# Two ResNet-style blocks in fp32: loads at the start, scale rows, V tiles by column pairs, a positions buffer and the last output chunk

## The chip, the cores and the metric

The kernel runs on one core of one Trainium2 chip. The time is the device time of one execution in microseconds (us). TensorE (PE) does the matmuls, VectorE (DVE) and ScalarE (ACT) the elementwise work, GpSimd (POOL) and SyncE (SP) mostly issue DMAs. ACT can issue DMAs too: an issue stands in its own queue, in order with its other work, so an issue that waits holds up the instructions behind it.

## The reference, cut to what matters

x has 16 images of 1024 channels and 32x32 pixels, all in fp32. Two layers follow each other.

```python
# layer 0
h = relu(bn(conv1x1(x, w_conv1)))                    # 1024 -> 256
q, k, v = relu(bn(conv1x1(h, wq))), relu(bn(conv1x1(h, wk))), bn(conv1x1(h, wv))
# per pixel, heads of 8 channels, 3x3 neighbourhood:
attn = softmax(sum_d q * (unfold3x3(k) + pos))       # 9 logits
h = relu(bn(sum_9 unfold3x3(v) * attn))
x = relu(bn3(conv1x1(h, w_conv3)) + x)               # 256 -> 1024, residual
# layer 1
o = relu(bn(conv1x1(x, w1)))                         # 1024 -> 256
o = relu(bn(conv3x3(o, w2)))                         # 256 -> 256
x = relu(bn(conv1x1(o, w3)) + x)                     # 256 -> 1024, residual
```

pos is pos_h + pos_w, one number per channel and neighbour. Each bn of layer 1 is a scale gamma / sqrt(var + eps) and a shift.

## The kernel before, in words

**Stages.** A list of stages (L917) sets the order of TensorE. For image b: C is layer 0's first convolution, Q the products for k and q and the position terms, V those for v. F is "fused": layer 0's last convolution, its residual, and at once layer 1's first convolution. W is the 3x3 convolution for a group of four images in Winograd form (W0, W4, W8, W12). U is layer 1's last convolution with its residual. The list begins P0 P1 P2 P3 F0 (P stands for C, Q, V) and ends W12 U11 U12 U13 U14 U15. In a stage of 1x1 convolution one chunk is 128 channels of one image, 512 KB, and its matmuls take about 3.4 us.

**VectorE.** The attention of an image (`attend`), the Winograd input transform of an image (`transform`) and, at the start, the Winograd form of w2 (`winograd_weights`, L251) and the folding of bn3's and layer 1's scales into the weights w3 and u3 (`scale_weights`) are jobs. A planner (class Side, L820) puts their instructions between those of the stages, by clocks of its own. Within an engine the resulting order is fixed.

**Queues.** SyncE issues the weights (`more_weights`, six buffers, in a fixed order), the stores of Winograd weights, of transformed images ("v") and of attention results. GpSimd issues the loads of x, of stored residuals and of V tiles (`more_loads`, L305: one list in fixed order, eight buffers, next when one is free), the stores of results (L397), of q (L490) and of the positions (L484). The eight x chunks of image 0 are issued on ACT's queue (L322). Each DMA takes a semaphore in turn, one of eight for SyncE and ACT together and one of eight for GpSimd, and its issue waits until the DMA before it on that semaphore has landed.

**What the change touches.**
- The beginning. L89 loads the parameters (`par`). L150 to L160 compute layer 1's norms from them (one square root on ACT, nine small operations on VectorE), L181 to L194 a small table of positions. Then `at_first` issues the x chunks of image 0, the taps of w2 and the unscaled w3 and u3 (GpSimd), four pieces of weights (SyncE: both halves of w1, the first in two parts, then wqk and wv), registers the two first jobs, and calls `scale_rows`.
- `scale_rows` (L217) brings the 1024 scales of each layer, which lie in SBUF as 128 partitions by 8 columns, into one row of 1024 that is the same in every partition: a store to DRAM with a transpose (1024 pieces of 4 bytes), then a load that reads the row 128 times ("scales"). `scale_weights` multiplies (L231) and stores the result.
- `winograd_weights` works on ACT and VectorE by turns (L259 to L270) and stores each row of products as `uw`; the stage Q of image 0 runs beside it.
- Q (`project`, L422): k and q are normed by ACT (L444) and stored. `positions` (L465) multiplies q with the position table (L470), lets ACT copy the sums from PSUM (L479) into q's first half, `q[:, 0, :]`, and stores them (L484). That copy overwrites q, so it waits until q's own store (L490) has read it.
- `transform` (L649) makes the six column forms of an image in three pairs, (1,2), (3,4), (0,5), each form in a zpool buffer, and stores them (L690) in DRAM. After an image's last pair it counts the image (`forms`), and a V tile is loaded once all four images are counted. V tiles are named (i, part); part 0 holds columns 1 and 3, part 1 columns 2 and 4, part 2 columns 0 and 5.
- zpool has three buffers: the scales, the forms v, the trees of the softmax and the copies z of a Winograd stage (L746) share them.
- `Expand.result` (L388) adds shift and relu to a chunk by one ACT operation over its 1024 pixels (L396) and stores it on GpSimd's queue (L397). The last chunk of all is chunk 7 of image 15.

Of the kernel before, what the change touches and what calls it, by code (L numbers as in the profile page):

```python
# [10 lines left out]
ALU = mybir.AluOpType  # L11
# [60 lines left out]
def sa_bottleneck_kernel(ctx: ExitStack, tc: tile.TileContext, x, w1t, wqkvt, w3t, u1t, u2t, u3t, params, out):  # L72
# [74 lines left out]
    bn_a = const.tile([P, _NBN], F32, tag="bn_a", name="bn_a")  # L147
    bn_r = const.tile([P, _NBN], F32, tag="bn_r", name="bn_r")
    bn_t = const.tile([P, _NBN], F32, tag="bn_t", name="bn_t")
    nc.vector.tensor_scalar(bn_a, bn_block("L1_conv_v1"), EPS, None, ALU.add)  # L150
    nc.scalar.activation(bn_r, bn_a, AF.Sqrt)

    nc.vector.reciprocal(bn_t, bn_r)
    nc.vector.tensor_mul(bn_t, bn_t, bn_a)
    nc.vector.tensor_add(bn_t, bn_t, bn_r)
    nc.vector.tensor_scalar(bn_t, bn_t, 0.5, None, ALU.mult)
    nc.vector.reciprocal(bn_r, bn_t)
    nc.vector.tensor_mul(bn_inv, bn_r, bn_block("L1_conv_g1"))
    nc.vector.tensor_mul(bn_t, bn_inv, bn_block("L1_conv_m1"))
    nc.vector.tensor_sub(bn_sh, bn_block("L1_conv_b1"), bn_t)  # L160


    members = const.tile([P, G], F32, tag="members", name="members")
# [14 lines left out]

    offsets = const.tile([P, NW, NPOS], F32, tag="offsets", name="offsets")
    pos = const.tile([P, NW, G, NPOS], F32, tag="pos", name="pos")  # L180
    for n in range(NW):  # L181
        for half, name in enumerate(("L0_conv_pos_h", "L0_conv_pos_w")):
            nc.vector.tensor_tensor(
                offsets[:, n, 2 * half : 2 * half + 2],
                col(name, 3 * n, 2),
                col(name, 3 * n + 2).to_broadcast([P, 2]),
                ALU.subtract,
            )
        nc.vector.tensor_tensor(
            pos[:, n],  # L190
            members.unsqueeze(2).to_broadcast([P, G, NPOS]),
            offsets[:, n].unsqueeze(1).to_broadcast([P, G, NPOS]),
            ALU.mult,
        )  # L194

# [19 lines left out]
    def scale_rows():  # L217

        for which, scale in enumerate((col("L0_conv_bn3_s", 0, NC), bn_inv[:, 2 * NW : 2 * NW + NC])):
            row = dram.tile([NC, P], F32, tag=f"row{which}", name="row")  # L220
            nc.sync.dma_start(row.rearrange("o p -> p o"), scale)
            t = zpool.tile([P, HW], F32, tag="z", name="scales")
            nc.sync.dma_start(t, AP(row.tensor, row.offset, [[0, P], [1, C]]))
            scales.append(t)

    def scale_weights():

        for which in range(2):
            for half in range(2):
                t = scaled[which, half]  # L230
                nc.vector.tensor_tensor(  # L231
                    t, t, scales[which][:, halves(half)].unsqueeze(1).to_broadcast([P, NW, HALF]), ALU.mult
                )
                nc.sync.dma_start(ws[which, half], t)
                yield 1.3


# [67 lines left out]
    def more_loads():  # L305

        while credits[0] and loads:
            kind, b, c = loads[0]
            if kind == "V":
                if forms.get(b, 0) < NK:  # L310
                    return
                src = form_room(b)[c[0], c[1]].rearrange("p k j e -> p (k j e)")
            elif kind == "r":
                if (b, c) not in stored:
                    return
                src = stored[b, c]
            else:
                src = x[b, c * P : (c + 1) * P, :]
            t = xpool.tile([P, NK * 2 * PART], F32, tag="x", name=f"{kind}_{b}_{c}".translate(str.maketrans(" ,", "__", "()")))
            t = t if kind == "V" else t[:, :HW]  # L320

            (nc.scalar if kind == "x" and b == 0 else nc.gpsimd).dma_start(t, src)  # L322
            loaded[loads.pop(0)] = t
            credits[0] -= 1
# [34 lines left out]
    class Expand:  # L359
# [28 lines left out]
        def result(self, o, to):  # L388
            t = self.tiles.pop(o)
            ps, to_ = self.ahead.pop(o), t  # L390

            if self.kind == "s":
                ps, to_ = ps.rearrange("p (n j) -> p j n", j=4), t.rearrange("p (j n) -> p j n", j=4)
            else:
                ps, to_ = ps.rearrange("p (j n) -> p n j", j=4), t.rearrange("p (n j) -> p n j", j=4)
            nc.scalar.activation(to_, ps, RELU, bias=self.shift(o), scale=1.0)  # L396
            nc.gpsimd.dma_start(to, t)  # L397
            return t
# [23 lines left out]
    def project(b):  # L422

        h = hidden.pop(b)

        def conv(which, n):
            ps = psum.tile([P, HW], F32, tag="ps", name="ps")
            name, at = ("wqk", which * WID) if which < 2 else ("wv", 0)
            key, at = piece(name, 0), at + n * P
            for half in range(2):  # L430
                for m in range(NW):
                    nc.tensor.matmul(  # L432
                        ps[:, halves(half)],
                        pieces[key][:, m, at : at + P],
                        h[:, m, halves(half)],
                        start=(m == 0),
                        stop=(m == NW - 1),
                    )
            if n == NW - 1 and which:
                done_with(key)  # L440
            return ps

        def norm(dst, src, name, n, func):
            nc.scalar.activation(  # L444
                dst, src, func,
                bias=col(f"L0_conv_{name}_b", n), scale=col(f"L0_conv_{name}_s", n),
            )

        def halo(name, which, func):

            room, backs[name] = by_quarter(name, b, HALO, HEAD_DIM)
            for n in range(NW):
                norm(inside(kp, n), rows(conv(which, n)), name, n, func)

                block = kp[:, n]
                nc.sync.dma_start(
                    room[n], AP(block.tensor, block.offset, [block.ap[0], [JROWS * PW, NJ], [1, HALO]])
                )
                yield CHUNK

        backs = relaid[b] = {}
        q = hpool.tile([P, NW, HW], F32, tag="h", name=f"q_{b}")
        room, backs["q"] = by_quarter("q", b, JPIX, HEAD_DIM)

        def positions():  # L465

            ps = psum.tile([P, HW], F32, tag="ps", name="ps")
            for half in range(2):
                for n in range(NW):
                    nc.tensor.matmul(  # L470
                        ps[n * G * NPOS : (n + 1) * G * NPOS, halves(half)],
                        pos[:, n].rearrange("p g t -> p (g t)"),
                        q[:, n, halves(half)],
                        start=True,
                        stop=True,
                    )

            by_offset = q[:, 0, :]
            nc.scalar.activation(by_offset, ps, AF.Identity)  # L479

            room, backs["pos"] = by_quarter("pos", b, JPIX, NPOS)
            by_offset = by_offset.rearrange("p (j w) -> p j w", j=NJ)
            for n in range(NW):
                nc.gpsimd.dma_start(room[n], by_offset[n * G * NPOS : (n + 1) * G * NPOS])  # L484

        k = halo("bnk", 1, RELU)
        yield next(k)
        for n in range(NW):
            norm(q[:, n, :], conv(0, n), "bnq", n, RELU)
            nc.gpsimd.dma_start(room[n], q[:, n, :].rearrange("p (j w) -> p j w", j=NJ))  # L490
            yield CHUNK
        yield next(k)
        positions()
        side.add(b)
        written.add(("qk", b))
        relay("qk", b)
        yield 2.5
        for n, cost in enumerate(halo("bnv", 2, AF.Identity)):
            if n:
                written.add(("v", b))  # L500
                relay("v", b)
            yield cost
# [146 lines left out]
    def transform(b, src):  # L649
# [35 lines left out]
        for make, two in pairs:  # L685
            v = [zpool.tile([P, HW], F32, tag="z", name="v")[:, : NI * PART] for _ in two]
            make([u.rearrange("p (l c) -> p l c", c=TR) for u in v], [t[:, :, at : at + TR] for at in PLACES])
            for j, u in zip(two, v):
                at = COLUMNS.index(j)
                nc.sync.dma_start(  # L690
                    room[:, at // 2, :, b % NK, at % 2].rearrange("i p e -> p i e"),
                    u.rearrange("p (i e) -> p i e", i=NI),
                )

            yield 4.3, 0.0 if b % NK == NK - 1 else 3.0
        forms[b - b % NK] = forms.get(b - b % NK, 0) + 1
        more_loads()

    def winograd_conv(b):

# [412 lines left out]
    made = []  # L1113

    def at_first():
        more_loads()
        for m in range(NW):
            load_taps(m)
        load_scaled()
        for _ in range(4):  # L1120
            more_weights()
        side.first(winograd_weights(), 24.0, 0.0)
        side.first(scale_weights(), 24.0, 0.0)
        scale_rows()
        hooks["conv1", 2, 0] = clear_hidden

    at_first()
# [42 lines left out]
```

## Time and profile before

The median of three runs is 2446.26 us (2446.19 to 2449.38). The profiled run took 2443.2 us, its span is 2441.2 us.

| engine | busy us | share | instructions |
|---|---|---|---|
| TensorE | 2388.6 | 98% | 6144 |
| VectorE | 2076.8 | 85% | 1631 |
| ACT | 918.2 | 38% | 873 |
| GpSimd | 463.2 | 19% | 851 |

A busy share is an average over all stages; where TensorE waits, and for whom, is told by the view of waits and by the timeline. In a timeline the columns are start, length, engine, line and operation, "out<-in", shapes, count, and in brackets the idle time before with what ended it. "q" behind an engine's name is its queue of DMA issues. Lines of one kind that follow each other are put together: "x8" are eight of them, and the length then spans all of them.

### The profile page before, as it was taken

Reading aid. Unit: us, or ns where it says so; the run is one execution under the profiler, and the core shown is the slowest. Engines: PE = TensorE matmul, PEld = TensorE weight load, DVE = VectorE, ACT = ScalarE, POOL = GpSimd, SP = SyncE. Lnnn points to the kernel's source line nnn. Section 1 sums busy time; section 2 is a strip of 40 time slices with the busy share of each in tenths; the row PEclk is TensorE's granted clock in tenths of the full one; section 3 lists DMA queues with packets and bytes.
Section 4 is the critical chain, followed back from the end, with each engine's and each line's share of the span. In section 5 each row is a group of like instructions: output and inputs, shape, how many; then the busy total and the mean of one; then the engine's idle time right before and its main releaser. Section 6 shows DMA issues by size and latency. Waiting matters only on the chain.

```text
span 2441.2 us, 18393 instructions
## 1 busy us (share of the span) xinstructions
PE 2388.6 (98%) x6144; PEld 1152.5 (47%) x6144; DVE 2076.8 (85%) x1631; ACT 918.2 (38%) x873; POOL 463.2 (19%) x851
## 2 busy tenths in 40 slices
PE   7999999999999999999999999999999999998998
PEld 3444444444466444444466444444466444434843
DVE  3899998999989999998989999899989999964700
ACT  2323142333122564433122564334222553443265
POOL 2121111111121222111111222111121221112122
PEclk9999999999999999999999999999999999999999
DMA  9967787878697899797888899797798897799788
GB/s 316 381 232 267 287 257 246 266 274 268 251 345 256 310 324 355 260 316 266 254 310 284 287 319 354 239 316 280 250 348 283 285 339 264 275 306 322 280 263 270
DMA packets 307693, 708.37 MB, mean 290 GB/s; under 512 B 22544, under 2 KB 176144, under 8 KB 298896
## 3 DMA queue, kind: packets, MB, share of 16 engines
q0 software_dynamic: 118816, 470.86, 54.4%
q1 hardware_dynamic: 187488, 232.10, 29.3%
q10 hardware_dynamic: 1296, 4.24, 0.5%
q8 instruction: 49, 0.80, 0.1%
q14 instruction: 44, 0.36, 0.0%
HBM read 432.10 MB, written 275.03 MB: 290 GB/s over the span
## 4 chain that ended last, share of the span: by engine, by line
PE 64%; DVE 15%; DMA 13%; issue 5%; ACT 2%; POOL 1%; SPq 0%; ACTq 0%; POOLq 0%; DVEq 0%
PE ps L346 26%; PE ps L377 19%; PE ps L432 10%; DMA out_dram<-r 8%; PE ps L723 8%; DVE acc L590 3%; DVE acc L603 3%; DVE prod L539 2%; DVE v L654 1%; DVE form L654 1%; DMA row<-par 1%; PE ps L470 1%; DVE prod L544 1%; DMA bnk<-kp 1%; POOL r L322 1%
## 5 line engine op out<-in xcount | busy, mean ns | idle before, releaser
L377 PE MATMUL ps<-a,w 128*128 128x512 f32 x1024 | 461.3, 596 | 4.9 <-ACT a L629 4.6
L346 PE MATMUL ps<-s,u 128*128 128x512 f32 x1024 | 458.3, 593 | 2.7 <-ACT s L396 2.7
L346 PE MATMUL ps<-x,w 128*128 128x512 f32 x1024 | 444.5, 595 | 14.2 <-DMA x<-in_x_dram 14.2
L377 PE MATMUL ps<-y,u 128*128 128x512 f32 x1024 | 442.6, 593 | 6.2 <-ACT ps L370 6.2
L590 DVE TENSOR_TENSOR acc<-e,bnv 128x2048 f32<-128x2048 f32 x144 | 327.5, 2284 | 3.6
L539 DVE TENSOR_TENSOR prod<-qc,bnk 128x2048 f32<-128x2048 f32 x144 | 324.1, 2287 | 1.7
L396 ACT ACTIVATE s<-ps,par 128x1024 f32<-128x1024 f32 x128 | 142.5, 1113 | 471.4 <-PE ps L377 402.9
L346 PEld LDWEIGHTS ps<-x,w 128*128 128x128 f32 x1024 | 195.5, 191 | 260.0 <-issue 259.0
L377 PEld LDWEIGHTS ps<-a,w 128*128 128x128 f32 x1024 | 195.3, 191 | 252.8 <-issue 242.2
L377 PEld LDWEIGHTS ps<-y,u 128*128 128x128 f32 x1024 | 194.2, 190 | 252.7 <-issue 236.4
L346 PEld LDWEIGHTS ps<-s,u 128*128 128x128 f32 x1024 | 194.7, 190 | 248.0 <-issue 237.9
L603 DVE TENSOR_TENSOR acc<-acc 128x2048 f32<-128x2048 f32 x128 | 293.4, 2292 | 4.4
L432 PE MATMUL ps<-h,wqk 128*128 128x512 f32 x512 | 225.9, 595 | 5.4 <-ACT h L975 5.2
L397 POOL DMA_DIRECT2D r<-s x128 | 68.6, 536 | 630.5 <-ACT s L396 600.4
L396 ACT ACTIVATE r<-ps,bn_sh 128x1024 f32<-128x1024 f32 x128 | 141.8, 1108 | 106.5 <-PE ps L377 106.1
L544 DVE TENSOR_TENSOR prod<-prod 128x2048 f32<-128x2048 f32 (+1 forms) x80 | 166.2, 2077 | 2.4
L432 PEld LDWEIGHTS ps<-h,wqk 128*128 128x128 f32 x512 | 96.2, 190 | 132.7 <-issue 109.9
L370 ACT ACTIVATE ps<-r 128x1024 f32<-128x1024 f32 x128 | 130.4, 1020 | 46.3 <-DMA r<-r 38.7
L975 ACT ACTIVATE h<-ps,par 128x1024 f32<-128x1024 f32 x32 | 38.5, 1203 | 278.1 <-PE ps L346 278.1
L370 ACT ACTIVATE ps<-s 128x1024 f32<-128x1024 f32 x128 | 131.2, 1025 | 22.8 <-DMA s<-in_x_dram 20.4
L444 ACT ACTIVATE kp<-ps,par 128x1024 f32<-128x1024 f32 x64 | 77.4, 1209 | 144.4 <-PE ps L432 127.8
L322 POOL DMA_DIRECT2D r<-r x128 | 68.1, 532 | 288.6 <-DMA out_dram<-r 176.1
(312 smaller groups left out, 2289.4 us busy)
## 6 DMA issues: line engine op xcount, KB each, us to landing
s<-in_x_dram POOLq DMA_DIRECT2D x128, 512.0 KB, 6.4
r<-s POOLq DMA_DIRECT2D x128, 512.0 KB, 4.9
r<-r POOLq DMA_DIRECT2D x128, 512.0 KB, 5.7
out_dram<-r POOLq DMA_DIRECT2D x128, 512.0 KB, 6.5
x<-in_x_dram POOLq DMA_DIRECT2D x120, 512.0 KB, 5.2
v<-v SPq DMA_DIRECT2D x96, 408.0 KB, 5.5
U<-uw SPq DMA_DIRECT2D x72, 512.0 KB, 6.0
bnk<-kp SPq DMA_DIRECT2D x32, 680.0 KB, 6.6
```

What stands on the lines that cost most here:

```text
L322: (nc.scalar if kind == "x" and b == 0 else nc.gpsimd).dma_start(t, src)
L346: nc.tensor.matmul(ps[n][:, halves(half)], wt[:, c % (NC // 2), n * P : (n + 1) * P], src[:, halves(half)], start=(c == 0), stop=(c == NC ...
L370: nc.scalar.activation(ps, t, AF.Identity)
L377: nc.tensor.matmul(self.ahead[o][:, halves(half)], pieces[key][:, n, o % (NC // 2) * P :][:, :P], self.src[:, n, halves(half)], start=Fals ...
L396: nc.scalar.activation(to_, ps, RELU, bias=self.shift(o), scale=1.0)
L432: nc.tensor.matmul(ps[:, halves(half)], pieces[key][:, m, at : at + P], h[:, m, halves(half)], start=(m == 0), stop=(m == NW - 1),)
L444: nc.scalar.activation(dst, src, func, bias=col(f"L0_conv_{name}_b", n), scale=col(f"L0_conv_{name}_s", n),)
L539: nc.vector.tensor_tensor(by_row(t[:, two]), by_row(qc), kc[:, :, i : i + JROWS, j : j + W], ALU.mult)
L544: nc.vector.tensor_add(u[:, :, 0:4], u[:, :, 0:4], u[:, :, 4:8])
L590: nc.vector.tensor_tensor(by_row(dst), rows(e[:, k, :]).unsqueeze(1).to_broadcast([P, HEAD_DIM, JROWS, W]), vc[:, :, i : i + JROWS, j : j ...
L603: nc.vector.tensor_add(acc, acc, t)
L723: nc.tensor.matmul(acc[i][:, at, :, n, :], pieces[key][:, m, at, n * P : (n + 1) * P], v[:, at, :, m * (TILES + TR) :][:, :, :TILES], star ...
```

## The change

It has five parts.

1. At the start the first piece of w1, then the x chunks of image 0 are issued before the norms (now a function `norms`); the other weights and the position table follow later.
2. The scale rows are written by partition, 128 pieces of 32 bytes, on GpSimd's queue, as is the load of the scales. The row's order is then permuted, and `scale_weights` reads it with a stride of 8.
3. A V tile waits only for the column pairs that it holds: parts 0 and 1 for pairs (1,2) and (3,4), part 2 for (0,5). GpSimd's queue gets W12's loads ahead of some output stores thereby; at the other Winograd stages its order stays.
4. The positions are copied into a zpool buffer of their own, so that the copy needn't wait for q's store.
5. The last chunk of the output is done half by ACT, half by VectorE, and stored in two halves on ACT's and SyncE's queues.

```diff
+    def norms():
...
+    def position_table():
...
     def scale_rows():
-            row = dram.tile([NC, P], F32, tag=f"row{which}", name="row")
-            nc.sync.dma_start(row.rearrange("o p -> p o"), scale)
+            row = dram.tile([P, NC], F32, tag=f"row{which}", name="row")
+            nc.gpsimd.dma_start(row, scale)
             t = zpool.tile([P, HW], F32, tag="z", name="scales")
-            nc.sync.dma_start(t, AP(row.tensor, row.offset, [[0, P], [1, C]]))
+            nc.gpsimd.dma_start(t, AP(row.tensor, row.offset, [[0, P], [1, C]]))
...
     def scale_weights():
         for which in range(2):
+            scale = scales[which].rearrange("p (m o) -> p o m", o=NC)
+            shape = [P, NW, NC // 2, P]
             for half in range(2):
-                t = scaled[which, half]
+                t = scaled[which, half].rearrange("p n (o m) -> p n o m", m=P)
                 nc.vector.tensor_tensor(
-                    t, t, scales[which][:, halves(half)].unsqueeze(1).to_broadcast([P, NW, HALF]), ALU.mult
+                    t, t, scale[:, half * NC // 2 :][:, : NC // 2].unsqueeze(1).to_broadcast(shape), ALU.mult
                 )
...
     def more_loads():
             if kind == "V":
-                if forms.get(b, 0) < NK:
+                if forms.get((b, c[1] == 2), 0) < NK:
                     return
...
     def result(self, o, to):
+            if (self.kind, self.b, o) == ("r", B - 1, NC - 1):
+                one, two = slice(0, JPIX // 2), slice(JPIX // 2, JPIX)
+                nc.scalar.activation(to_[:, one], ps[:, one], RELU, bias=self.shift(o), scale=1.0)
+                nc.vector.tensor_scalar(to_[:, two], ps[:, two], self.shift(o), 0.0, ALU.add, ALU.max)
+                nc.scalar.dma_start(to[:, :HALF], t[:, :HALF])
+                nc.sync.dma_start(to[:, HALF:], t[:, HALF:])
+                return t
...
         def positions():
-            by_offset = q[:, 0, :]
+            by_offset = zpool.tile([P, HW], F32, tag="z", name="by_offset")
             nc.scalar.activation(by_offset, ps, AF.Identity)
...
     def transform(b, src):
+            if two != (1, 2):
+                key = b - b % NK, two == (0, 5)
+                forms[key] = forms.get(key, 0) + 1
+                more_loads()
             yield 4.3, 0.0 if b % NK == NK - 1 else 3.0
-        forms[b - b % NK] = forms.get(b - b % NK, 0) + 1
-        more_loads()
...
     def at_first():
+        more_weights()
         more_loads()
+        norms()
         for m in range(NW):
             load_taps(m)
         load_scaled()
-        for _ in range(4):
+        scale_rows()
+        for _ in range(3):
             more_weights()
+        position_table()
         side.first(winograd_weights(), 24.0, 0.0)
         side.first(scale_weights(), 24.0, 0.0)
-        scale_rows()
         hooks["conv1", 2, 0] = clear_hidden
```

More of the change, by code (lines that the diff above doesn't have):

```diff
@@ L149, in sa_bottleneck_kernel @@
     bn_t = const.tile([P, _NBN], F32, tag="bn_t", name="bn_t")
[L150 to L160, printed above, removed]
+    def norms():
+        nc.vector.tensor_scalar(bn_a, bn_block("L1_conv_v1"), EPS, None, ALU.add)
+        nc.scalar.activation(bn_r, bn_a, AF.Sqrt)
+        nc.vector.reciprocal(bn_t, bn_r)
+        nc.vector.tensor_mul(bn_t, bn_t, bn_a)
+        nc.vector.tensor_add(bn_t, bn_t, bn_r)
+        nc.vector.tensor_scalar(bn_t, bn_t, 0.5, None, ALU.mult)
+        nc.vector.reciprocal(bn_r, bn_t)
+        nc.vector.tensor_mul(bn_inv, bn_r, bn_block("L1_conv_g1"))
+        nc.vector.tensor_mul(bn_t, bn_inv, bn_block("L1_conv_m1"))
+        nc.vector.tensor_sub(bn_sh, bn_block("L1_conv_b1"), bn_t)
     members = const.tile([P, G], F32, tag="members", name="members")
@@ L180, in sa_bottleneck_kernel @@
     pos = const.tile([P, NW, G, NPOS], F32, tag="pos", name="pos")
-    for n in range(NW):
-        for half, name in enumerate(("L0_conv_pos_h", "L0_conv_pos_w")):
+    def position_table():
+        for n in range(NW):
+            for half, name in enumerate(("L0_conv_pos_h", "L0_conv_pos_w")):
+                nc.vector.tensor_tensor(
+                    offsets[:, n, 2 * half : 2 * half + 2],
+                    col(name, 3 * n, 2),
+                    col(name, 3 * n + 2).to_broadcast([P, 2]),
+                    ALU.subtract,
+                )
             nc.vector.tensor_tensor(
[L184 to L187, printed above, removed]
-            )
[L189 to L194, printed above, removed]
+                pos[:, n],
+                members.unsqueeze(2).to_broadcast([P, G, NPOS]),
+                offsets[:, n].unsqueeze(1).to_broadcast([P, G, NPOS]),
+                ALU.mult,
+            )
     kp = const.tile([P, NW, H + 2, PW], F32, tag="kp", name="kp")
@@ L228, in scale_weights @@
         for which in range(2):
+            scale = scales[which].rearrange("p (m o) -> p o m", o=NC)
+            shape = [P, NW, NC // 2, P]
             for half in range(2):
-                t = scaled[which, half]
+                t = scaled[which, half].rearrange("p n (o m) -> p n o m", m=P)
                 nc.vector.tensor_tensor(
-                    t, t, scales[which][:, halves(half)].unsqueeze(1).to_broadcast([P, NW, HALF]), ALU.mult
+                    t, t, scale[:, half * NC // 2 :][:, : NC // 2].unsqueeze(1).to_broadcast(shape), ALU.mult
                 )
-                nc.sync.dma_start(ws[which, half], t)
+                nc.sync.dma_start(ws[which, half], scaled[which, half])
                 yield 1.3
```

## The prediction

> **What bounds the kernel now.** I read the busy shares first, then TensorE's waits, then the timeline at each place where TensorE waited.
>
> ```profile
> PE 2388.6 (98%) x6144; PEld 1152.5 (47%) x6144; DVE 2076.8 (85%) x1631; ACT 918.2 (38%) x873; POOL 463.2 (19%) x851
> ```
>
> TensorE is busy in 2388.6 of 2441.2 us. Its 6144 instructions are untouched by the change, and they run in the same order. So only the other 52.6 us can go[...].
>
> ```profile
> PE ps L346 <- DMA x<-in_x_dram: 14.2, 1, 14.2
> PE ps L723 <- issue: 6.8, 1, 6.8
> ...
> PE ps L432 <- ACT h L975: 5.2, 12, 0.4
> PE ps L377 <- ACT a L629: 4.6, 2, 3.4
> PE ps L723 <- ACT z L746: 3.4, 2, 3.2
> PE ps L470 <- ACT q L444: 2.8, 2, 1.6
> ```
>
> The columns are total, times and longest. Three of these are single events: 14.2 at the start, 6.8 in one Winograd stage, 3.2 in another.
>
> ```profile
> 3.31 0.47 SPq L221 DMA_DIRECT2D row<-par  x1
> 3.48 27.73 ACTq L322 DMA_DIRECT2D x<-in_x_dram  x8
> 14.20 30.09 PE L346 MATMUL ps<-x,w 128*128 128x512 f32 x64 [14.20 <-DMA x<-in_x_dram]
> 30.36 0.34 SPq L223 DMA_DIRECT2D scales<-row  x1
> 31.26 0.84 ACT L259 ACTIVATE g<-g 128x768 f32<-128x768 f32 x1 [27.58 <-DMA row<-par]
> 32.13 1.83 DVE L263 SCALAR_TENSOR_TENSOR g<-g 128x768 f32<-128x768 f32 x2 [14.95 <-ACT g L259]
> 43.09 2.44 ACT L975 ACTIVATE h<-ps,par 128x1024 f32<-128x1024 f32 x2
> ```
>
> That is the start: the first chunk of x is issued at 3.48 and matmuls begin at 14.20. ACT stands for 27.58 us, because the issue of x chunk 6 sits in its queue and takes a semaphore that the write of the first scale row (4 KB, 27.0 us to land in the DMA view) still holds.
>
> ```profile
> 2240.07 0.54 POOL L322 DMA_DIRECT2D V__0_8009<-v  x1 [0.16 <-issue]
> 2248.14 6.72 PE L723 MATMUL ps<-V__0_8009,U 128*128 128x256 f32 x16 [6.83 <-issue]
> 2254.70 3.62 PE L723 MATMUL ps<-V__0_8011,U 128*128 128x256 f32 x16
> ```
>
> This is the last Winograd stage, W12: its first V tile is issued at 2240.07, TensorE is ready at 2241.31, and the matmuls start at 2248.14.
>
> ```profile
> 2435.14 1.11 ACT L396 ACTIVATE r<-ps,bn_sh 128x1024 f32<-128x1024 f32 x1 [2.32 <-PE ps L377]
> 2435.70 0.53 POOL L397 DMA_DIRECT2D out_dram<-r  x1 [3.24 <-issue]
> 2436.56 0.53 POOL L397 DMA_DIRECT2D out_dram<-r  x1 [0.33 <-ACT r L396]
> ```
>
> The tail: the last matmul ends at 2435.05, then come one ACT pass over a whole chunk and one store, landed at 2440.04.
>
> [...]the row write, 1024 packets of 4 bytes, took 27.0 us while a 512 KB load issued beside it took about 7.[...]after 6.83 us of wait the 16 matmuls took 6.72 us, against 3.62 for the next 16; after a 3.19 us wait they took 3.72.
>
> **The change, part by part.**
>
> *x ahead of the norms.* Before, ACT's queue did the sqrt table load (1.28 us at 1.24) and the sqrt (3.47, waiting for VectorE) before its first x issue at 3.48; now x is issued after the parameters' issue, about 1.25. In SyncE's queue only the first half of w1 (512 KB) is certainly ahead, not all 1.8 MB of weights; x's packets began at 7.5 before, once those had drained. Bytes needed for the first matmul: 512 KB of w1 and 512 KB of x, 2.6 us at the 400 GB/s of this stretch, after about 2.0 us of latency (the first 64 KB of w1, issued at 0.81, took 2.2 to land): 0.8 + 2.0 + 2.6 = 5.4; the first matmul needs only those 64 KB of w1, so I take 5.2, against 14.20. So −9.0; bounds 4.5 (x alone) to 8 (x waits for other weights). Later pieces come in time: [...]x chunks 6 and 7, needed at 28.5 and 31.9, are issued near 20 and land at 26 to 30.
>
> The first conv thus ends near 35.1 instead of 44.29. But something takes its place. The sqrt now stands behind all eight x issues, and the last is free near 20 (it waits for a semaphore of x chunk 1). Then: table load 1.28, sqrt 0.25, eight norms 2.0, position table 0.9, VectorE's L261 1.0: L263 begins at about 25, instead of 32.13. ACT's h (L975) came 10.95 us after L263 (43.09 − 32.13), behind the weight work in its queue: 36.1, and done for the first half at 37.3. The next stage wants it at 35.1, so 2.2 of the 9.0 come back: qk starts 7.0 us earlier (bounds 5 to 9.2).
>
> *Rows by partition on GpSimd's queue.* Four DMAs leave SyncE's queue, where the first Winograd-weight store waited behind them until 46.0; a row is now 128 pieces of 32 bytes instead of 1024 of 4. In qk the position matmuls (L470) waited 1.15 + 1.64 us for ACT's q, itself behind the weight stages that waited for those stores (ACT 8.65 at 54.78, VectorE 9.72); [...]the position stage ended at 65.95, where 44.32 + 16 matmul groups' 13.7 + 1.94 = 59.98 was possible: 5.97 lost. With the stores free from about 32 I take 4.5 back (3 to 6). Against it: x of image 1 is now issued behind the rows on GpSimd's queue, near 35 instead of 20.34; it is needed near 61 and takes under 10 to land: nothing. VectorE, whose attention starts at 95.92, gains 16 us of lead.
>
> *Strided scale reads (L231).* Four operations of 1.22 us. The stride is not in the trace; [...]on VectorE, which has the 16 us of lead: nothing.
>
> *A buffer of its own for positions.* ACT's L479 waited for the store of q at 700.89 (8.92 us), and behind it in ACT's queue the copy z (L746) held TensorE 3.19 us at 702.88. The tile now comes from the three zpool buffers, whose last users on VectorE had ended 18 us or more earlier: −3.2 (2 to 3.2). The added wait: whoever takes that buffer next waits for the positions' store, 5.8 us to land. The tightest are VectorE's transform operations after images 4 and 7 (326.5 to 335.97, 588.9 to 597.1: 3.6 and 2.5 us to spare). So nothing, if landings stay below 8.
>
> *Columns by pairs.* The first two V tiles now wait only for the stores of pairs (1,2) and (3,4), and jump ahead of four output stores in GpSimd's queue. Image 15's pair (3,4) is issued at 2230.96 and 2232.0 and lands 4.5 later: V issued at 2236.5 instead of 2240.07. At 6 to 8 us for the landing it is there at 2242.5 to 2244.5: TensorE waits 1.2 to 3.2 instead of 6.83[...]. About −4 −3 = −7 (3 to 8.5). Output chunks held 5 us longer free buffers that the later V tiles need; those have 3.6 us a tile to catch up: nothing.
>
> *Last chunk split.* ACT's half takes about 0.6 instead of 1.11, VectorE's half follows it, and the two stores of 256 KB go on idle queues: −1.0. The floor is the chunk before it, still issued at 2435.70 and landed at 2438.6: at most −1.4.
>
> Sum: −7.0 −4.5 −3.2 −7.0 −1.0 = −22.7; 2446.3 − 22.7 = 2423.6.
>
> **The rivals.**
> *A. ACT and VectorE hold the early part* (weight chain no earlier than before[...]). For it: h depends on a queue that now starts its weight work only after x 7. Against it: 27.58 us of standing fall to about 20. Start and qk together −3, the rest −11.2: about 2432.
> *B. The weights chain keeps up*, h is never waited for, and the whole 9 + 6 come: −26 to −27, about 2419. For it: ACT's h has 10 us of queue before it in which much was waiting. Against it: the sqrt is behind eight issues.
> *C. The late gains fail*: V lands no earlier, since its transfer collides with image 15's last stores and output; then −11.5 −3.2 + 4 = −10.7, about 2436. For it: V took 8.0 to land with those stores around it.
> *D. Slower.* The new users of zpool tie VectorE's transforms and softmax trees to GpSimd's stores: the 2.5 us of slack is used up in most of 16 images at 2 us each, +30, or image 1 waits for x behind the rows, against −23: about 2452. For it: the slack is small, and VectorE is 85% busy. Against it: VectorE is 16 us ahead of TensorE's need from the start, and store landings in the page are steady.
>
> **How the numbers follow.** Forecast 50%, A 20%, B 18%, C 6%, D 6%. The forecast's own bounds are 5 + 3 + 2 + 3 + 0.4 = 13.4 and 9.2 + 6 + 3.2 + 8.5 + 1.4 = 28.3, so 2418 to 2433 if all err together. Range 2414 to 2437, holding A and B and most of C. Faster (by over 4.9 us) 0.88: all but D and a part of C; same 0.06; slower 0.06.
>
> **What would show it.** Right: first matmul at 5 to 6; the L470 waits gone or under 1; no z wait at 703; V of W12 issued near 2236.5[...]; last landing about 1 us after the one before it. Wrong: a wait for h (L975) of over 4 us after the first conv, new waits of x in it, VectorE waits on the positions' store at L665 or L753 that move TensorE, or the V issue still behind a late store.

## The result, and the profile after

The changed kernel takes 2434.91 us, median of four runs (2432.54 to 2436.8), beside 2446.72 for the kernel before: a ratio of 0.9949 (0.9932 to 0.9966), so 11.8 us less, of which 22.7 had been forecast. A second measurement gave 0.9955 (0.9936 to 0.9973). Single executions of one kernel differ by 10 us and more (2442 to 2462 for the kernel before in that measurement), so ratios carry the verdicts here, and a trace of one execution tells where time goes, not how much of it on average.

The page of the changed kernel, its row of busy shares: TensorE's work is what it was.

```profile
PE 2388.0 (98%) x6144; PEld 1150.9 (47%) x6144; DVE 2080.7 (85%) x1632; ACT 918.9 (38%) x873; POOL 466.2 (19%) x854
```

TensorE's waits in the changed kernel (total, times, longest):

```profile
PE ps L385 <- ACT ps L378: 15.6, 7, 6.6
PE ps L448 <- ACT h L992: 10.5, 13, 5.2
PE ps L354 <- DMA x<-in_x_dram: 6.3, 1, 6.3
PE ps L385 <- ACT a L644: 3.0, 2, 2.7
PE ps L354 <- ACT s L412: 2.2, 1, 2.2
PE ps L486 <- ACT q L460: 1.5, 1, 1.5
PE ps L740 <- DMA U<-uw: 1.4, 1, 1.4
PE ps L740 <- ACT z L763: 0.3, 1, 0.3
```

The three single events that the change aimed at are gone or smaller: 14.2 at the start is 6.3, 6.8 in W12 is gone (with a new wait of 1.4 there, for the next weights U), and 3.2 in W0 is 0.3. But two rows have grown: the wait for seeds (L378, the residual that ACT copies into PSUM) from 6.5 to 15.6, and the wait for h (L992) from 5.2 to 10.5, with one wait of 5.2 in it that was not there.

The start, in the timeline of the changed kernel:

```profile
1.24 14.82 ACTq L330 DMA_DIRECT2D x<-in_x_dram  x8
6.25 29.15 PE L354 MATMUL ps<-x,w 128*128 128x512 f32 x64 [6.25 <-DMA x<-in_x_dram]
16.09 1.28 ACT L153 ACT_TABLE_LOAD   x1 [16.09 <-DMA x<-in_x_dram]
21.21 1.83 DVE L270 SCALAR_TENSOR_TENSOR g<-g 128x768 f32<-128x768 f32 x2
```

x is issued at 1.24, matmuls begin at 6.25, ACT is free at 16.09 and the weight chain reaches its first long sum (L263 before, L270 now) at 21.21 instead of 32.13. After image 0 TensorE is 11.9 us ahead of the kernel before. Then, at image 2 (three timelines of the changed kernel, VectorE, ACT and TensorE; lines between those shown are left out):

```profile
84.78 3.94 DVE L238 TENSOR_TENSOR vh<-vh,scales 128x1024 f32<-128x1024 f32 x2
88.63 3.94 DVE L238 TENSOR_TENSOR scaled<-scaled,scales 128x1024 f32<-128x1024 f32 x2
92.49 4.50 DVE L554 TENSOR_TENSOR prod<-qc,bnk 128x2048 f32<-128x2048 f32 x2
```

```profile
141.58 2.12 ACT L586 ACTIVATE e<-e 128x2304 f32<-128x2304 f32 x1 [20.83 <-DVE e L583]
143.61 2.28 ACT L992 ACTIVATE h<-ps,par 128x1024 f32<-128x1024 f32 x2
```

```profile
129.59 10.03 PE L354 MATMUL ps<-x,w 128*128 128x512 f32 x23
144.85 7.52 PE L448 MATMUL ps<-h,wqk 128*128 128x512 f32 x12 [5.23 <-ACT h L992]
```

The same place in the kernel before, ACT and VectorE:

```profile
91.38 2.35 DVE L231 TENSOR_TENSOR vh<-vh,scales 128x1024 f32<-128x1024 f32 x2
95.92 4.49 DVE L539 TENSOR_TENSOR prod<-qc,bnk 128x2048 f32<-128x2048 f32 x2
145.01 2.12 ACT L571 ACTIVATE e<-e 128x2304 f32<-128x2304 f32 x1 [17.31 <-DVE e L568]
149.85 1.20 ACT L975 ACTIVATE h<-ps,par 128x1024 f32<-128x1024 f32 x1 [2.72 <-PE ps L346]
```

ACT waits 20.83 us for VectorE's logits before image 0's exp, and image 2's h stands behind that exp in ACT's queue; TensorE waits 5.23 us for h. The exp came at 145.01 before, so VectorE, from here the slower of the two, is only 3.4 us ahead; and before, h still waited for TensorE (2.72).

W12, TensorE's and GpSimd's timelines of the changed kernel:

```profile
2242.45 3.62 PE L740 MATMUL ps<-V__0_7995,U 128*128 128x256 f32 x16
2245.91 3.62 PE L740 MATMUL ps<-V__0_7997,U 128*128 128x256 f32 x16
2250.94 3.69 PE L740 MATMUL ps<-V__1_7999,U 128*128 128x256 f32 x16 [1.41 <-DMA U<-uw]
```

```profile
2235.48 0.54 POOL L330 DMA_DIRECT2D V__0_7995<-v  x1 [4.61 <-DMA v<-v]
2236.00 0.54 POOL L330 DMA_DIRECT2D V__0_7997<-v  x1
2236.97 0.53 POOL L330 DMA_DIRECT2D V__1_7999<-v  x1 [0.43 <-issue]
```

The first V tile is issued at 2235.48, no wait stands ahead of the first matmuls, and 16 of them take 3.62 us, not 6.72 (mean granted clock 1.00 in that stretch, 0.53 before). But TensorE comes to them only at 2242.45. In the kernel before it was ready at 2241.31, so in these two traces nothing of the early lead is left when W12 begins.

The tail, from the timelines of ACT, VectorE and SyncE:

```profile
2428.99 0.69 ACT L407 ACTIVATE r<-ps,bn_sh 128x512 f32<-128x512 f32 x1 [1.80 <-issue]
2429.71 0.35 ACTq L409 DMA_DIRECT2D out_dram<-r  x1
2429.72 0.75 DVE L408 TENSOR_SCALAR r<-ps,bn_sh 128x512 f32<-128x512 f32 x1 [113.52 <-ACT r L407]
2430.49 0.34 SPq L410 DMA_DIRECT2D out_dram<-r  x1
```

The halves run one after the other (0.69 and 0.75); the two half stores take 2.5 and 2.4 us to land, where the whole one took 3.5. From the last matmul's start to the end of the execution it is 5.7 us, 6.8 before.

### The profile page after: what moved, and what is told of

It reads as the page before. It is cut to its first block, busy times and chain, and to the rows that moved or that the text cites. A ratio compares the mean times of both kernels' runs of the same rounds, so it can differ in the third digit from the quotient of the medians.

```text
span 2434.0 us, 18415 instructions
## 1 busy us (share of the span) xinstructions
PE 2388.0 (98%) x6144; PEld 1150.9 (47%) x6144; DVE 2080.7 (85%) x1632; ACT 918.9 (38%) x873; POOL 466.2 (19%) x854
## 3 DMA queue, kind: packets, MB, share of 16 engines
q10 hardware_dynamic: 1440, 4.51, 0.5%
## 4 chain that ended last, share of the span: by engine, by line
PE 72%; DMA 11%; issue 5%; DVE 3%; POOL 2%; ACT 1%; SPq 0%; POOLq 0%; ACTq 0%; DVEq 0%
PE ps L354 32%; PE ps L385 21%; PE ps L448 11%; PE ps L740 7%; DMA out_dram<-r 7%; DMA bnk<-kp 1%; DMA U<-uw 1%; POOL r L330 1%; PE ps L486 1%; DVE acc L605 1%; DMA s<-in_x_dram 1%; DVE acc L618 1%; ACT h L992 0%; DMA pos<-by_offset 0%; POOL out_dram L413 0%
## 5 line engine op out<-in xcount | busy, mean ns | idle before, releaser
L448 PE MATMUL ps<-h,wqk 128*128 128x512 f32 x512 | 227.8, 599 | 10.5 <-ACT h L992 10.5
L378 ACT ACTIVATE ps<-r 128x1024 f32<-128x1024 f32 x128 | 130.5, 1022 | 68.9 <-DMA r<-r 61.4
L992 ACT ACTIVATE h<-ps,par 128x1024 f32<-128x1024 f32 x32 | 38.4, 1204 | 272.5 <-PE ps L354 248.1
L378 ACT ACTIVATE ps<-s 128x1024 f32<-128x1024 f32 x128 | 131.2, 1025 | 22.4 <-DMA s<-in_x_dram 20.0
```

The costliest lines, as they stand in the source:

```text
L378: nc.scalar.activation(ps, t, AF.Identity)
L448: nc.tensor.matmul(ps[:, halves(half)], pieces[key][:, m, at : at + P], h[:, m, halves(half)], start=(m == 0), stop=(m == NW - 1),)
```

## The experiments

Theory A: the early lead is lost at the exp, where TensorE meets VectorE. Theory B: the stages U1 to U3 with F4 (850 to 950 us) and U5 to U7 with F8 (1427 to 1520 us) take a lead back, whatever made it. Ratios are to the kernel before, measured beside each kernel; the brackets are 95% intervals. The first four kernels, on one chip, without the changed kernel beside them:

Scale operations later:

```diff
-        side.first(scale_weights(), 24.0, 0.0)
+        side.first(scale_weights(), 120.0, 0.0)
-        hooks["conv1", 2, 0] = clear_hidden
+        hooks["conv1", 3, 0] = clear_hidden
```

> The changed kernel, with the four scale operations on VectorE moved behind the first softmax's maximum (and the clearing of vh one image later). Theory A, the early lead is lost at image 0's exp, which stands in ACT's queue ahead of image 2's h and waits for VectorE: the wait of 5.2 us for h at 145 falls under 1, TensorE is 11 to 12 us ahead of the kernel before from there (5.4 in the changed kernel), and the end comes 6 us earlier than the changed kernel: about 2429. Theory B, the stages U2, U3 and U7 take back any lead, because their output stores wait behind the attention's loads: the h wait goes too, but the end stays at 2434 to 2436.

Measured 0.9918 (0.9898 to 0.9938). ACT's timeline in this kernel:

```profile
135.63 2.12 ACT L586 ACTIVATE e<-e 128x2304 f32<-128x2304 f32 x1 [18.11 <-DVE e L583]
139.42 1.21 ACT L992 ACTIVATE h<-ps,par 128x1024 f32<-128x1024 f32 x1 [1.67 <-PE ps L354]
```

The exp comes 6.0 us earlier, and h waits for TensorE, not the other way round: the mechanism of A is shown. In all 14 traces of this study image 0's exp starts 49.1 to 49.2 us after VectorE begins the attention, so what delays that beginning delays the exp. What the edit is worth in the end is another matter (see the second measurement below).

The beginning alone (diff: parts 1 and 2 of the change only):

> The kernel before with the new beginning alone (x ahead of the norms, scale rows by partition on GpSimd's queue, strided scale reads); columns, positions buffer and last chunk as before. Theory A: TensorE is 11.9 us ahead at image 0's q, 5.4 at image 2's, and keeps it: about 2441.5. Theory B: the lead is gone after the first group's U stages, so 2445 to 2447.

Measured 0.9980 (0.9971 to 0.9990): 5.1 us of the 11.9. That is theory A's figure and not B's. Its trace doesn't show a lead that is kept, though: TensorE is 5.3 us ahead of the kernel before's first trace at image 2's q, 4.3 before W0 and 0.6 after it, where this kernel waits 4.7 us for ACT's copy z.

The late parts alone (parts 3, 4 and 5 only):

> The kernel before with the V tiles by column pairs, the positions buffer and the split last chunk; the beginning as before. Theory A: W0 gives 3, W12 8 to 9.5, the tail 1, and all stays: about 2434. Theory B: the 3 of W0 are taken back in the U stages that follow, the 8 to 9.5 and the 1 behind the last U stages of that kind stay: about 2437.

Measured 0.9962 (0.9947 to 0.9976): 9.4 us. This is B's figure, 2437 where A said 2434, but A's (0.995) lies in the interval too. Within the intervals the two halves of the change add up: 5.1 + 9.4 = 14.5 against 11.8 to 12.8 measured for the whole.

Output stores of layer 1 on SyncE's queue:

```diff
-            nc.gpsimd.dma_start(to, t)
+            (nc.sync if self.kind == "r" else nc.gpsimd).dma_start(to, t)
```

> The changed kernel with the output stores of layer 1 issued on SyncE's queue instead of GpSimd's. Theory B: the waits for seeds in U3 and U7 (6.6 and 5.3 us in the changed kernel) fall under 2, as the output stores no longer stand behind the attention's loads: about 2424 to 2428. Theory A says nothing of these waits; if they come from the transfers sharing the engines rather than from their order in one queue, they stay, and the time is 2433 to 2437.

Measured 0.9871 (0.9852 to 0.9890), lower than the changed kernel's 0.995 and than the 0.991 to 0.992 expected. The wait in U3 falls to 1.4 us; in the second group waits of 2.6 and 2.8 us remain, where under 2 was expected. What the edit acts on is seen in GpSimd's timeline of the changed kernel, and in ACT's (the last line):

```profile
890.30 0.54 POOL L330 DMA_DIRECT2D r<-r  x1 [2.74 <-DMA out_dram<-r]
890.83 0.54 POOL L535 DMA_DIRECT2D qc<-q  x1
891.35 0.53 POOL L535 DMA_DIRECT2D bnk<-bnk  x1
891.88 0.53 POOL L535 DMA_DIRECT2D pc<-pos  x1
892.40 0.54 POOL L413 DMA_DIRECT2D out_dram<-r  x1
893.60 0.53 POOL L330 DMA_DIRECT2D r<-r  x1 [0.67 <-DMA out_dram<-r]
894.13 0.54 POOL L413 DMA_DIRECT2D out_dram<-r  x1
906.01 0.53 POOL L330 DMA_DIRECT2D r<-r  x1 [11.35 <-DMA out_dram<-r]
907.00 1.03 ACT L378 ACTIVATE ps<-r 128x1024 f32<-128x1024 f32 x1 [9.89 <-DMA r<-r]
```

An output store (892.40) and a residual load (893.60) follow the attention's three loads, 2.9 MB, in the same queue. Both land 13.3 us after their issue, the residual load at 906.92; ACT makes the seed from it at 907.00, and TensorE waits 6.60 us, until 908.08. The next residual load (906.01) stands still for 11.35 us until a store's landing frees its buffer.

With the stores on SyncE's queue such a store lands 9.9 us after its issue, ahead of the three loads (10.9, 14.9 and 16.8). A residual load behind the three still takes 16.1 us. But TensorE comes to the chunk that needs it 20.2 us after the first of the three was issued, where it was 10.7 in the changed kernel. So the residual loads run further ahead of TensorE, and it waits little (TensorE's timeline in this kernel):

```profile
904.45 1.12 PE L385 MATMUL ps<-y,u 128*128 128x512 f32 x2 [1.36 <-ACT ps L378]
```

Two things may help here, that stores land sooner and so free buffers, and that GpSimd's loads no longer stand behind the issues of stores; this run moves both at once and doesn't tell them apart.

The second four, on one chip:

> The changed kernel itself, beside the three others on one chip, so that they can be compared with it. Theory A and B alike: 0.995 of the kernel before. In its trace the wait of about 5 us for image 2's h comes again, and waits for seeds in U3 and U7 that sum to over 8 us; if these sums differ from the first trace's by several us, they are chance of a single execution and no effect of the change.

Measured 0.9955. The h wait is there (5.6), and the seeds' waits too (17.5 us in all, 6.4 and 4.1 of it the longest in U3 and U7): they are no chance of one execution.

The positions again in q (the diff undoes part 4):

```diff
-            by_offset = zpool.tile([P, HW], F32, tag="z", name="by_offset")
+            by_offset = q[:, 0, :]
```

> The changed kernel with the positions again copied into q's first half. Prediction's step: 3 us at W0 come back, so 3 us slower than the changed kernel (0.996 of before). Theory B: the 3 us are taken back in the U stages anyway, so the same as the changed kernel within 1 us. If the buffer's added waits cost VectorE anything, it is faster.

Measured 0.9954 (0.9938 to 0.9970), beside the changed kernel's 0.9955: no difference is seen, as B said, but with intervals of about ±4 us each the 3 us are not ruled out either. In W0 this kernel waits 3.6 us and the changed one 0.3 and 2.5; in the changed kernel ACT's copy z there waits 5.09 and 7.30 us for the positions' store, whose buffer it takes over, so part of the old wait has only changed its name.

Both edits, later scales and stores on SyncE's queue:

> The changed kernel with both the scale operations behind the first maximum and layer 1's output stores on SyncE's queue. Theory A: the 6 us of the h wait come on top of the stores' gain, so about 6 us faster than the stores alone (0.985 of before). Theory B, in the form that VectorE sets the pace of the later stages: no faster than the stores alone (0.987).

Measured 0.9887 (0.9863 to 0.9911): no faster than the 0.9871 of the stores alone, which was measured on another chip, so B's figure as far as that comparison goes.

Scale rows transposed, but on GpSimd's queue, without strided reads:

```diff
-            row = dram.tile([P, NC], F32, tag=f"row{which}", name="row")
-            nc.gpsimd.dma_start(row, scale)
+            row = dram.tile([NC, P], F32, tag=f"row{which}", name="row")
+            nc.gpsimd.dma_start(row.rearrange("o p -> p o"), scale)
```

> The changed kernel with the scale rows written transposed again (1024 pieces of 4 bytes) but on GpSimd's queue, so that the four scale operations read without a stride. If the stride (7.9 against 4.7 us in all) is one half of what holds the exp, the h wait falls from 5.2 to about 2 us and TensorE leads by about 8.5 us at image 2; if the stride is nothing, 5.2 stays.

One execution: 2442.40. The expectation missed. The four scale operations do take 4.7 us instead of 7.9, but the row stores take 23.6 and 15.1 us to land (16.1 and 5.0 by partition), and TensorE waits in two new places (its timeline in this kernel):

```profile
55.50 1.32 PE L483 MATMUL ps<-q,pos 128*64 128x512 f32 x2 [4.44 <-ACT q L457]
57.89 3.67 PE L483 MATMUL ps<-q,pos 128*64 128x512 f32 x6 [1.07 <-ACT q L457]
101.72 8.65 PE L445 MATMUL ps<-h,wqk 128*128 128x512 f32 x13 [4.88 <-ACT h L989]
```

The whole lead of the start is gone at 101.72, where the kernel before came at 100.5. So in this trace the early x alone is not enough; the rows by partition keep its gain, and the stride's 3.2 us are less than what they save. The total of a single execution says nothing here.

The last four, on one chip, repeat the kernels whose size was open:

> The kernel before itself, for a second trace. Theory B (the change makes the U stages lose more): the waits of the two groups U0 to U3 and U4 to U7, with the fused stage behind each, again sum to about 8 us, against 16 to 19 in the changed kernel's two traces. Theory C (the first trace of before was a lucky execution; the sums are chance and the change has no part in them): they sum to 11 to 17. The ratio is 1.000.

Measured 1.0007 (0.9996 to 1.0019). The sums of the two groups' waits are 9.8 us (5.8 and 4.0), 7.9 in the first trace: below the 11 to 17 that chance would have needed, so the change makes these stages lose more. Of the variants, the beginning alone and the positions in q have 12.2 us each, the late parts alone 16.1.

> The changed kernel with the scale operations behind the first maximum, a second time, beside the others on one chip. Theory A: 0.992 to 0.993 of before, that is 6 us under the changed kernel's 0.995. Theory B: 0.995.

Measured 0.9948 (0.9930 to 0.9965): B's figure. This interval and that of the first measurement (0.9898 to 0.9938) hardly overlap; between nothing and 6 us the gain of this edit alone stays open.

> The changed kernel with layer 1's output stores on SyncE's queue, a second time, beside the others on one chip: 0.987 to 0.990 of before, with waits in the two U groups of under 5 us together. This and the next run differ only in the place of the scale operations.

Measured 0.9930 (0.9912 to 0.9947), less than the gain expected, with 6.0 us of waits in the two groups, a little over the expected 5. That the waits go is seen again; the size of the gain differs between the two measurements by 0.006.

> Both edits together, a second time. Theory A: 6 us (0.0025) under the run with the stores alone, beside it on the same chip. Theory B: equal to it within 2 us.

Measured 0.9914 (0.9894 to 0.9934), median 2424.08 beside 2428.45 for the stores alone: 4.4 us, on A's side, but the two intervals overlap, so this isn't settled. TensorE's waits in it:

```profile
PE ps L354 <- DMA x<-in_x_dram: 6.1, 1, 6.1
PE ps L448 <- ACT h L992: 5.7, 13, 0.4
PE ps L740 <- DMA U<-uw: 3.0, 1, 3.0
PE ps L740 <- issue: 2.9, 1, 2.9
PE ps L385 <- ACT ps L378: 2.8, 4, 1.0
```

The seeds' waits are 2.8 us in all. This kernel has the shortest medians of the study, 22.5 and 28.7 us under the kernel before in its two measurements.

The traces at one glance: when TensorE reached the same five instructions (us). The four with a star ran on a chip on which the kernel before takes 2457.8 us (median), the others where it takes 2446.6 to 2450.6, so the differences between two columns of a row tell more than a column.

| kernel | image 2, q | after W0 | F4 | F8 | W12, end |
|---|---|---|---|---|---|
| before | 154.6 | 816.9 | 949.9 | 1517.0 | 2299.6 |
| before, again | 154.3 | 816.1 | 953.5 | 1521.5 | 2303.3 |
| beginning alone * | 149.4 | 816.3 | 954.2 | 1525.1 | 2307.8 |
| late parts alone * | 154.7 | 815.3 | 954.3 | 1532.7 | 2304.6 |
| changed | 149.6 | 809.3 | 949.6 | 1521.4 | 2292.5 |
| changed, again | 151.0 | 812.9 | 955.2 | 1529.2 | 2299.3 |
| positions in q | 146.5 | 812.9 | 951.0 | 1522.9 | 2296.1 |
| later scales * | 144.2 | 812.8 | 958.2 | 1531.0 | 2305.1 |
| later scales, again | 143.1 | 809.2 | 949.0 | 1522.8 | 2291.7 |
| stores on SyncE * | 150.3 | 811.3 | 940.6 | 1510.7 | 2285.9 |
| stores on SyncE, again | 148.7 | 809.9 | 940.5 | 1508.2 | 2286.3 |
| rows transposed | 158.0 | 820.5 | 958.7 | 1528.1 | 2300.4 |
| both edits | 145.2 | 808.1 | 938.5 | 1502.2 | 2274.9 |
| both edits, again | 142.9 | 808.3 | 937.7 | 1500.4 | 2275.2 |

Between the second and third columns the kernels with stores on GpSimd's queue need 133 to 145 us, those with stores on SyncE's 129 to 131. Pair by pair, the changed kernel's traces come to W0's end 3 to 8 us ahead of the kernel before's, are within 2 us of them at F4 and 4 to 8 us behind at F8. This is no fixed exit time: "later scales, again" came at 809 and left at 949, "rows transposed" came at 820 and left at 959. From the first to the second column the 6.7 us between "changed" and "later scales" (means 150.3 and 143.7) have shrunk to nothing (811.1 and 811.0); between the two "again" traces, on one chip, half of 7.9 us is left.

## Why the prediction was right in its direction, and where it was not

The direction was right, the gain half of the forecast. 2434.9 lies above the forecast's own bounds (2418 to 2433) and in the range only because that was drawn wide enough for rival A and most of C. A's figure (2432) is the nearest, but its mechanism, a weight chain no earlier than before, did not occur, and C's (V lands no earlier) did not either: that the range held is in part luck. This is how far TensorE was ahead of the kernel before (us, minus for behind), in the first traces of the two kernels and in their second ones:

| pair | image 0 | image 2, q | after W0 | F4 | F8 | ready for W12 | W12, end | end |
|---|---|---|---|---|---|---|---|---|
| first | 11.9 | 5.0 | 7.6 | 0.3 | −4.4 | −1.1 | 7.1 | 7.2 |
| second | 11.0 | 3.3 | 3.2 | −1.7 | −7.7 | −2.5 | 4.0 | 5.5 |

In both pairs all that is left at the end was won in W12 and the tail. These executions end 5.5 and 7.2 us apart, the medians 11.8 and 12.8; no trace shows the rest.

*Start and qk: right in sum.* Forecast −7.0 and −4.5; the traces show −8.9 and −3.0. x took 6.25, not 5.2 (the first piece of w1 is 128 KB, not 64); but ACT was free at 16.09, not 20, and L270 began at 21.21, not 25, so the 2.2 us of wait for h never came. The errors cancel. The load of image 1, moved from 20.34 to 36.82 (forecast 35), was hidden, as said. The mechanism of the forecast's rival B (the weight chain keeps up) was the true one here, its total was not. Of the waits at L470, 1.5 of 2.8 us remain. Part of the 5.97 us that the forecast read there is slower matmuls: six took 3.37 us at a mean granted clock of 0.55 (62.58 to 65.88), where in the changed kernel six take 1.93 us at 1.00 (52.32 to 54.25). One reading of the kernel before fits only in part, without effect on the sum: of the loads beside the first row store, those of x took 10.6 us and more to land, not about 7.

*The step that failed is the one that says "on VectorE, which has the 16 us of lead: nothing".* There TensorE lost about 7 us. The strided reads cost 7.9 − 4.7 = 3.2 us; the trace of the kernel before did not show what a stride costs, and 16 us of lead would have covered these. But the lead was wrong; the forecast gives no sum for its 16 us. VectorE began the scale operations at 84.78, 6.6 us earlier than the 91.38 before, since the waits for stores of Winograd weights still lay in its chain (17.1 us in all, 16.4 before), and its attention began at 92.49, 3.4 earlier. From there its only pauses of note until image 4 are 2.2 us behind each exp. Before, it had 2.7 us to spare at the exp (exp's end at 147.13, h at 149.85). So of 11.9 us TensorE could keep 3.4 + 2.7 = 6.1. In the trace it begins image 2's q 6.5 us ahead, and 5.0 are left after the next few matmuls: after the wait of 5.23 us the first five take 0.94 to 1.22 us each (mean granted clock 0.50 from 144.85 to 149.00), the others 0.59 (0.98 from 149.00 to 152.40). The wait for h of over 4 us, which the forecast named as a sign of being wrong, did come, two images later than it was looked for. So far rival A was right: ACT and VectorE do hold the early part.

*Moving the strided operations shows the same bound from the other side.* Image 0's exp came 6 us sooner, image 1's hardly (238.5 and 237.4, against 238.9 in the changed kernel): by then VectorE has done the same work. TensorE's 6.7 us went at the next meetings, among them 2.8 and 1.9 us near 330, where ACT waited for the store of k's padded image, and 3.1 and 2.4 in W0.

*W0: mechanism right, its worth in the end open.* The wait of 3.2 us is 0.3 in the first trace and 2.5 in the second. The term put at nothing, that whoever takes the buffer next waits for the positions' store, was not nothing: this store takes 10.5 to 13.4 us to land there, where the forecast counted on 5.8 and at most 8, and ACT's copy z waits 5.09 and 7.30 us for it. Still, against the first trace of the kernel before, the two traces with the new beginning and the positions in q lose 3.6 and 3.4 us of their lead in W0, while the changed kernel gains 2.6 and 0.4 (all nine traces with the new beginning and the buffer: from 2.9 lost to 2.6 gained). In the total, no gain of the buffer was seen.

*W12 and the tail: right.* Forecast −7.0, of which 3 were an estimate from the trace of the kernel before, 6.72 us for the 16 matmuls after the wait against 3.62 for the next 16; the stores of pair (3,4) had landed 3.2 and 3.6 us after their issue there, not 4.5. The wait falls from 6.8 and 6.3 to 1.4 and 1.3, now for the weights U, and the stretch around it takes 82.7 us where it took 91.1 and 89.2, so −6.5 to −8.5. Forecast −1.0 for the tail; 5.7 and 5.3 instead of 6.8.

*What had no step: the U stages.* The forecast left their waits unchanged. They rose from 7.9 and 9.8 us to 16.1 and 18.7. The longest wait, in U3, shows how a lead is spent: it ends 1.2 us after the landing of the residual load that stands behind the attention's loads, and that landing follows the issue of those loads, which did not move ahead as far as TensorE did (in the first pair 4.4 us against 6.9; in the second it came 1.3 later, TensorE 1.3 sooner). In the ten traces with all stores on GpSimd's queue it comes 14.2 to 16.7 us after the first of those loads was issued. TensorE comes 13.2 to 13.7 us after that issue with the old beginning (three traces), 10.1 to 11.7 with the new one (seven), and waits 2.4 to 4.0 against 3.7 to 6.6 us. That accounts for 4.2 and 2.6 us of the rise in the two pairs of traces, not for all of it: the late parts alone, with the old beginning, also wait 16.1 us in the two groups, though on the chip where the kernel before takes 2457.8. Whether the positions buffer or the new order of the V loads adds to the waits was not tested alone.

In sum, the first pair of traces misses 15.5 us of the 22.7: about 7 at the exp, with the matmuls after it, and about 9 in the stages between W0 and W12; smaller differences cancel. The medians miss 10.9. How these divide is open: the beginning alone measures 5.1 us (2.5 to 7.1) at the end, so over many executions some of the early lead does seem to arrive.

## What to carry to other kernels

A lead that one engine gains is worth no more than the lead of the engine that it meets next plus the slack at that meeting (here 3.4 + 2.7 of 11.9 us); read that slack at the first meeting after the edit. Before counting a gain made early, look for waits in the middle whose end doesn't move with the engine that waits, such as a load that stands behind other transfers in one queue (here 13.3 us to land). Where short-lived buffers are filled and freed through the same queue as bulk loads, try another queue for one of the two; here, with the stores on SyncE's queue, the ratio was 0.987 and 0.993 where the changed kernel's was 0.995.

## What the hardware showed

Of two stores of 1024 scales, 1024 pieces of 4 bytes took 27.0 and 14.8 us to land on SyncE's queue and 23.6 and 15.1 on GpSimd's, 128 pieces of 32 bytes 16.1 and 5.0: with fewer pieces they landed sooner, while the queue made little difference; the traffic beside them was not the same. VectorE's multiplication of 128x1024 takes 1.97 us where one source is read with a stride of 32 bytes, 1.18 without (3.94 and 2.35 for two that follow each other): 1.9 ns a column against 1.15.

In the kernel before, the 16 matmuls after the wait of 6.83 us in W12 took 6.72 us at a mean granted clock of 0.53 (2248.14 to 2254.70), those after the wait of 3.19 us in W0 3.72 us at 1.00. Six matmuls at L470 ran at 0.55 after waits of only 1.15 and 1.64 us; what lowers the clock was not shown.

The waits for semaphores in the kernel before: GpSimd's first eight DMAs were issued from 3.35 to 7.40, the ninth stood 4.51 us until 12.64, and the first had landed at 12.35. On ACT's queue the issue of x chunk 6 stood until 30.36; the row store, issued at 3.31, took 27.03 us to land, until 30.34.
